# Conditional residual convolutions on one core: the weight products regrouped to eighteen blocks, VectorE's part of S in one form, the residual's identity scaled by ScalarE, and part of G placed ahead of S

## The chip, the cores and the metric

One of the eight cores of one Trainium2 chip runs the kernel. The metric is device time in microseconds (us), the median of several executions; less is better. All numbers are float32.

## What is computed

The reference adds to `x` (128 samples, 64 channels, length 1024) the result of four modulated convolutions of width 3:

```python
s = style @ mw.T + mb                       # per sample, per input channel
weight = SCALE * w * s[:, None, :, None]
demod = rsqrt(sum(weight * weight, axis=(2, 3)) + EPS)
weight = weight * demod[:, :, None, None]
# layers: 'same', 'upsample' (transposed conv, then a 4-tap blur), 'same', 'downsample' (blur, stride 2)
...
return x + chain_of_four_layers(x, cond, weights, biases, mod_w, mod_b)
```

All four layers are linear, so for each sample they amount to one convolution with nine taps of 64 x 64 and a constant; only the first and last three positions differ.

## The kernel before

The 128 samples are taken in 32 units of four samples (`NQ` = 32). A unit's two pairs lie on the two halves of the partitions, and two samples of each half on the two halves of TensorE's columns, so each product is issued as four matmuls of 64 x 64, one for each quarter of the array; "a product" below means these four. Each float32 matmul appears twice in the trace, as two passes.

For each unit the nine taps are built in a chain on TensorE, with a scaled copy after each link:

- `scale3`: ScalarE scales layer 3's weights into `wd` (five blocks of 64 columns: three taps and two sums).
- S (`stage1_a`, `stage1_b`): layer 2's weights times `wd` into the PSUM tile `psS`. ScalarE copies four blocks to `S` after part a; after part b VectorE adds the sums to two blocks (L442) and GpSimd finishes a third (L445). `share_sums` (L462, VectorE) adds blocks of `S` in pairs.
- R (`stage2`, `stage2_rest`): the blurred layer 1 (`E`, nine taps; `Ed`, differences of them) times `S` into `psR`. Some products are common to two blocks of R; they are made apart (`share`, into the free columns behind 340 of a unit's convolution bank `psA`) and copied into `psR` by ScalarE, each to two blocks (`share_copy`, L490), on top of which the rest is accumulated. ScalarE copies `psR` to `R`, GpSimd adds sums of neighbours (`r_sums`, L588).
- W (`stage3_b`, `stage3_a`): layer 0's weights times `R`, part b into a `psA` bank pair that isn't in use yet and part a into `psW`; ScalarE copies to `Wf`, nine blocks, one for each tap.
- H (`combine_a`, `combine_b`): VectorE makes the three combinations of taps that a fast convolution of three outputs with five products (numbered 0 to 4) needs (L662), and `residual` (L659) adds the scaled identity for `x + ...`.

`psS`, `psR` and `psW` are successive uses of one PSUM tile (`ps_w`, one buffer): whoever writes the next waits until the last was read.

The input's side: `G` (`in_g2`, `in_g01`: VectorE, L662) and `T` (`in04`, L740, and `in3`, L711: VectorE; `in1`, L726, and `in2`, L731: GpSimd) are sums of the input's three planes. The convolution itself is five products of three groups each, 340 columns wide (L753): product 3, 1 and 2 into `psA`, 4 into the PSUM tile `Y`, and 0 into the `psA` of the unit. `copy_m3`, `sum1` and `sum2` (VectorE; `sum2` writes `Y` in two steps of 340) form the three output planes, which ScalarE scales (`output`, L830) and SyncE stores.

The order is written out by hand: `turn_of(q)` for q = 4 to 28 works on four units at a time (q's outputs, n = q + 1, c = q + 2, s = q + 4), and each engine executes its instructions in the order of that code. Turns 5 to 27 use `share` (`sharing`). Most turns carry a small side task of VectorE (`SIDE`): one step of 384 to 576 columns in turns 8, 9, 11, 12, 16, 17 and 20 to 27, two or four small ones in turns 5, 6, 7, 10, 13, 15 and 18. Turns 10, 14, 15 and 19 also have products for the edges on TensorE (`SLOTS`), turns 4 to 6 a small constant product (`small`).

Of the kernel before, what the change touches and what calls it, by code (L numbers as in the profile page):

```python
# [63 lines left out]
def kernel(  # L64
# [199 lines left out]
    def var_newton(bs, ls=slice(0, NL)):  # L264
# [5 lines left out]
    tA, tB, tBn, tC, t0, t3, td, tb = (  # L270
        const.tile([P, NQ, 2], F32, name=n) for n in ("tA", "tB", "tBn", "tC", "t0", "t3", "td", "tb")
# [94 lines left out]
    w2n = const.tile([P, 5, C], F32, name="w2n")  # L366

    def split_weights():
        nc_g.tensor_copy(w3x[:, :K], w3)
        nc_g.tensor_scalar_mul(w2n[:, :K], woi[2], -1.0)  # L370
        for t, src in ((w3x, w3), (w2n, woi[2])):
            nc_g.tensor_add(t[:, K:], src[:, : K - 1], src[:, 1:])
# [32 lines left out]
    EVEN = slice(0, K, 2)  # L405

    def stage1(q, pool=None, engs=(nc_a, nc_a), between=None):

        wd = chain[q]
        ps = unit(pool or ps_w, f"psS{q}")  # L410
        for k, (at, at1) in enumerate(((0, 3), (3, 1), (1, 4))):
            tap_matmul(ps, wd, at, 2, woi[2][:, k, :], EVEN, first=k == 0)
            tap_matmul(ps, wd, at1, 1, woi[2][:, k, :], slice(1, 2), last=k == K - 1)
        if between:
            between()
        st, _ = s_tiles(q)
        for r in range(2):
            scaled_copy(engs[r], flat(st[r][:, 1:6]), ps[r][:, : 5 * C], tB[:, q, r : r + 1])
        chain[q] = st
        return ps  # L420

    def stage1_a(q, ps=None):
# [3 lines left out]
        tap_matmul(ps, wd, 2, 2, w2n[:, 0, :], EVEN, first=True)  # L426
        tap_matmul(ps, wd, 3, 2, w2n[:, 2, :], EVEN)
        tap_matmul(ps, wd, 1, 1, w2n[:, 1, :], slice(1, 2))
        st, t = s_tiles(q)
        for r in range(2):  # L430
            scaled_copy(nc_a, flat(st[r][:, :4]), ps[r][:, C : 5 * C], tBn[:, q, r : r + 1])
        chain[q] = wd, ps, st, t

    def stage1_b(q):

        wd, ps, st, t = chain[q]
        tap_matmul(ps, wd, 2, 1, w2n[:, 3, :], slice(3, 4))
        tap_matmul(ps, wd, 4, 1, w2n[:, 4, :], slice(4, 5), last=True)
        for r in range(2):
            p1 = st[r][:, 0:1, :].to_broadcast([P, 2, C])  # L440
            sums = ps[r][:, 2 * C : 6 * C].rearrange("c (a b o) -> c a b o", a=2, b=2)[:, :, 0]
            nc_v.scalar_tensor_tensor(  # L442
                st[r][:, 4:6, :], sums, tB[:, q, r : r + 1], p1, op0=ALU.mult, op1=ALU.subtract
            )
        nc_g.tensor_add(t[:, :, 2], t[:, :, 2], t[:, :, 0])  # L445
        chain[q] = st
        whole[q] = t

    whole, shared_ps = {}, {}
# [3 lines left out]
    def tap_differences():  # L453
# [4 lines left out]
        nc_g.tensor_sub(Ed[:, 4:], E[:, 3:8:4], E[:, 5:6].to_broadcast([P, 2, C]))  # L458

    def share_sums(q):  # L460
        t = whole[q]
        nc_v.tensor_add(t[:, :, 6:8], t[:, :, 1:5:3], t[:, :, 2:6:3])  # L462
# [13 lines left out]
    def share(q, ps):  # L476

        at = [NB + 4 + i * C for i in range(3)]
        p12, p34 = ([b[:, i:j] for b in ps] for i, j in zip(at, at[1:]))
        chain_matmul(p12, E[:, 2], chain[q], slice(6, 7))  # L480
        chain_matmul(p34, E[:, 6], chain[q], slice(6, 7))
        chain_matmul(p34, E[:, 5], chain[q], slice(7, 8), True)
        shared_ps[q] = [b[:, at[0] : at[2]] for b in ps]

    def share_copy(q):

        ps = unit(ps_w, f"psR{q}")
        for r in range(2):
            src = shared_ps[q][r].rearrange("c (a o) -> c a o", a=2)
            nc_a.copy(  # L490
                ps[r][:, C : 5 * C].rearrange("c (a b o) -> c a b o", a=2, b=2),
                src[:, :, None, :].to_broadcast([P, 2, 2, C]),
# [3 lines left out]
    def stage2_rest(q):  # L496

        ps = shared_ps.pop(q)
        block = lambda i, n=1: [b[:, i * C : (i + n) * C] for b in ps]
        apart = [b[:, : 4 * C].rearrange("c (a b o) -> c a b o", a=2, b=2)[:, :, 0] for b in ps]  # L500
        plan = (
            (apart, E[:, 0], slice(1, 4, 2)),
            (block(1), Ed[:, 0], slice(2, 3)),
            (block(2), Ed[:, 1], slice(1, 2)),
            (block(3), E[:, 2], slice(3, 4)),
            (block(3), Ed[:, 2], slice(2, 3)),
            (block(4), Ed[:, 3], slice(1, 2)),
            (block(4), E[:, 4], slice(3, 4)),
            (block(5, 2), E[:, 8], slice(2, 4)),
            (block(5), E[:, 6], slice(3, 4)),  # L510
            (block(1, 2), E[:, 1], slice(4, 6)),
            (block(2), E[:, 3], slice(4, 5)),
            (block(3), Ed[:, 4], slice(5, 6)),
            (block(4), Ed[:, 5], slice(4, 5)),
            (block(5), E[:, 7], slice(5, 6)),
# [5 lines left out]
    def stage2(q, pool=None, engs=(nc_a, nc_a), between=None):  # L521
# [28 lines left out]
    TAPS = slice(3, 9, 2), slice(4, 9, 2), slice(0, 3)  # L550
# [1086 lines left out]
```

## Time and profile before

| | |
|---|---|
| runs | 480.28, 480.38, 481.21 us; median 480.38 |
| profiled execution | span 478.0 us; its own time is not given beside the span |
| granted TensorE clock | 0.997 |
| TensorE matmul busy | 469.6 us (98%) |
| VectorE busy | 417.5 us (87%) |
| ScalarE busy | 310.1 us (65%) |
| GpSimd busy | 163.5 us (34%) |

The span runs from the first to the last instruction. The shares are means over the whole span, and a matmul counts as busy until its modelled end, so 98% does not say that nothing waits. What a turn can be is read from one turn's rows.

### The profile page before, as it was taken

How to read it: one execution, taken by the hardware profiler on the slowest of the kernel's cores; microseconds unless marked ns; L12 is line 12 of the kernel's file. 1: busy time of each engine (PE TensorE's matmuls, PEld its weight loads, DVE VectorE, ACT ScalarE, POOL GpSimd, SP SyncE). 2: the span in 40 equal slices, each digit the busy share in tenths (PEclk: the TensorE clock that was granted, in tenths of full speed). 3: DMA queues.
4: the chain of work that ended last, by engine and by line, in shares of the span. 5: the costliest groups of instructions: out<-in, count | busy, mean ns of one | idle time of the engine just before them, and what ended most of it. 6: DMA issues, size and time to landing. Idle time of an engine off the chain costs nothing.

```text
span 478.0 us, 26721 instructions
## 1 busy us (share of the span) xinstructions
PE 469.6 (98%) x11928; PEld 346.4 (72%) x11928; DVE 417.5 (87%) x690; ACT 310.1 (65%) x708; POOL 163.5 (34%) x197
## 2 busy tenths in 40 slices
PE   8999999999999999999999999999999999999995
PEld 7877788777878876677776677766887777766652
DVE  5889998879889998899979899979989999999895
ACT  5565666667666676666667666667666768766352
POOL 3434032663335342243432233422434432333200
PEclk9999999999999999999999999999999999999998
DMA  5406365544445554345543455533455554445125
GB/s 175 158 28 200 114 195 192 150 139 144 139 150 157 173 173 127 122 151 160 171 149 120 131 170 152 173 127 126 145 169 162 162 154 146 152 146 170 61 91 191
DMA packets 50514, 70.70 MB, mean 148 GB/s; under 512 B 5664, under 2 KB 47328, under 8 KB 50400
## 3 DMA queue, kind: packets, MB, share of 16 engines
q1 hardware_dynamic: 49808, 68.32, 45.8%
q8 instruction: 93, 1.52, 1.5%
q10 hardware_dynamic: 592, 0.69, 0.5%
q14 instruction: 21, 0.17, 0.1%
HBM read 35.36 MB, written 33.62 MB: 144 GB/s over the span
## 4 chain that ended last, share of the span: by engine, by line
PE 95%; DVE 4%; issue 0%; ACT 0%; ACTq 0%; DVEq 0%
PE psA L753 45%; PE Y L753 11%; PE psR L467 9%; PE psA L571 7%; PE psW L571 7%; PE psS L389 6%; PE psR L533 4%; PE psA L467 2%; PE Y L994 2%; DVE H L662 1%; PE Y L180 1%; PE Y L336 1%; DVE G L662 0%; PE psM L204 0%; DVE o L832 0%
## 5 line engine op out<-in xcount | busy, mean ns | idle before, releaser
L753 PE MATMUL psA<-T,H 64*64 64x340 f32 x2304 | 187.3, 447 | 0.8 <-DVE y L662 0.7
L753 PEld LDWEIGHTS psA<-T,H 64*64 64x64 f32 x2304 | 89.9, 133 | 50.0 <-issue 3.1
L662 DVE SCALAR_TENSOR_TENSOR G<-X 128x1376 f32<-128x1376 f32 (+2 forms) x65 | 78.1, 1207 | 1.1 <-DMA X<-in_x 0.9
L726 POOL TENSOR_TENSOR T<-G 128x684 f32<-128x684 f32 x28 | 46.5, 1659 | 73.1 <-DVE G L662 73.1
L445 POOL TENSOR_TENSOR S<-S 128x128 f32<-128x128 f32 x28 | 22.1, 790 | 144.1 <-ACT S L360 136.8
L360 ACT ACTIVATE R<-psR,tC 128x448 f32<-128x448 f32 x63 | 36.5, 630 | 46.3 <-PE psR L467 26.7
L753 PE MATMUL psA<-T,Wf 64*64 64x340 f32 x768 | 63.9, 446 | 0.0
L753 PE MATMUL Y<-T,Wf 64*64 64x340 f32 x768 | 62.8, 451 | 0.1
L662 DVE SCALAR_TENSOR_TENSOR Y<-m,psA 128x340 f32<-128x340 f32 x64 | 33.1, 517 | 28.0 <-PE psA L753 26.6
L360 ACT ACTIVATE psW<-psA 128x128 f32<-128x128 f32 x100 | 19.3, 269 | 50.3 <-PE psA L571 46.2
L740 DVE TENSOR_TENSOR T<-G 128x1368 f32<-128x1368 f32 (+1 forms) x33 | 50.7, 1540 | 0.0
L360 ACT ACTIVATE Wf<-psW,t 128x256 f32<-128x256 f32 (+2 forms) x76 | 32.7, 479 | 26.5 <-PE psW L571 26.2
L711 DVE TENSOR_TENSOR T<-X 128x684 f32<-128x684 f32 x32 | 47.9, 1496 | 0.0
L467 PE MATMUL psR<-S,E 64*64 64x64 f32 (+1 forms) x1472 | 46.5, 238 | 0.0
L731 POOL TENSOR_TENSOR T<-G 128x684 f32<-128x684 f32 x28 | 46.5, 1660 | 0.0
L389 PEld LDWEIGHTS psS<-wd,w2n 64*64 64x64 f32 x1120 | 35.0, 133 | 13.3 <-ACT S L360 0.8
L467 PEld LDWEIGHTS psR<-S,E 64*64 64x64 f32 x1472 | 39.6, 134 | 5.2 <-ACT psR L490 0.2
L753 PEld LDWEIGHTS Y<-T,Wf 64*64 64x64 f32 x768 | 29.6, 132 | 18.0 <-DVE Y L662 0.7
L830 ACT ACTIVATE o<-psA,tb,td 128x340 f32<-128x340 f32 x63 | 37.0, 647 | 6.3 <-PE psA L753 6.3
L753 PEld LDWEIGHTS psA<-T,Wf 64*64 64x64 f32 x768 | 29.1, 133 | 15.1
L830 ACT ACTIVATE o<-Y,tb,td 128x340 f32<-128x340 f32 x63 | 36.6, 637 | 4.5 <-PE Y L753 2.7
L830 ACT ACTIVATE o<-y,tb,td 128x340 f32<-128x340 f32 x62 | 38.5, 679 | 0.6 <-DVE y L812 0.6
(165 smaller groups left out, 832.4 us busy)
## 6 DMA issues: line engine op xcount, KB each, us to landing
out<-o SPq DMA_DIRECT2D x167, 170.0 KB, 2.6
X<-in_x SPq DMA_DIRECT2D x150, 172.0 KB, 3.6
X<-in_x SPq DMA_DIRECT2D x14, 516.0 KB, 5.3
out<-o SPq DMA_DIRECT2D x6, 510.0 KB, 5.4
out<-o SPq DMA_DIRECT2D x2, 340.0 KB, 3.0
Xe<-in_x_ends SPq DMA_DIRECT2D x1, 512.0 KB, 6.7
out<-o ACTq DMA_DIRECT2D x3, 170.0 KB, 2.3
par<-in_params SPq DMA_DIRECT2D x2, 192.0 KB, 3.4
```

The lines of the kernel that those rows point to most:

```text
L360: nc_a.activation(dst, src, AF.Copy, scale=f)
L389: nc.tensor.matmul(ps[r][cols, at * C : (at + n) * C], weight[rows], wd[c if r == 0 else 1 - c][rows, taps], start=first, stop=last, skip_ ...
L445: nc_g.tensor_add(t[:, :, 2], t[:, :, 2], t[:, :, 0])
L467: nc.tensor.matmul(dst[r][cols], weight[rows], st[c if r == 0 else 1 - c][rows, slots, :], start=False, stop=last, skip_group_check=True,)
L571: nc.tensor.matmul(dst[r][cols], weight[rows], t[rows, c, slots, :], start=first, stop=last, skip_group_check=True,)
L662: nc_v.scalar_tensor_tensor(out, x, f, y, op0=ALU.mult, op1=op)
L711: nc_v.tensor_sub(t[:, pairs, 0, :NJ], plane(X, 3, pairs), plane(X, 1, pairs))
L726: eng.tensor_add(t[:, :, 0, :NJ], plane(g, 2), plane(g, 1))
L731: eng.tensor_sub(t[:, :, 1, :NJ], plane(g, 2), plane(g, 1))
L740: nc_v.tensor_sub(t[:, pairs, :, :NJ], both(a, PL), both(b, 1))
L753: nc.tensor.matmul(ps[s][cols, :NB], w, Ts[q, tag][rows, c, i, g : g + NB], start=(g == 0 and m == 3), stop=(g == K - 1), skip_group_check ...
L830: nc_a.activation(dst, src, AF.Identity, bias=add, scale=d3)
```

## The change

The diff, cut to what the prediction speaks of. Blocks of `S` lie in another order (their slots), signs that were in `w2n` and `tBn` go to `En` (negated odd taps of `E`), `Wf` has its taps in natural order, and the PSUM tiles of R start one block further on.

```diff
     def stage1_b(q, eng=nc_v):
...
         for r in range(2):
-            p1 = st[r][:, 0:1, :].to_broadcast([P, 2, C])
-            sums = ps[r][:, 2 * C : 6 * C].rearrange("c (a b o) -> c a b o", a=2, b=2)[:, :, 0]
+            at = slice(3, 6, 1 if eng is nc_v else 2)
+            sums = blocks(ps, at)[r]
+            n = sums.shape[1]
+            p1 = st[r][:, 0:1, :].to_broadcast([P, n, C])
             nc_v.scalar_tensor_tensor(
-                st[r][:, 4:6, :], sums, tB[:, q, r : r + 1], p1, op0=ALU.mult, op1=ALU.subtract
+                st[r][:, at, :], sums, tB[:, q, r : r + 1], p1, op0=ALU.mult, op1=ALU.add
             )
-        nc_g.tensor_add(t[:, :, 2], t[:, :, 2], t[:, :, 0])
+        if eng is not nc_v:
+            eng.tensor_add(t[:, :, 4], t[:, :, 4], t[:, :, 0])
...
     def share(q, ps):
-        at = [NB + 4 + i * C for i in range(3)]
+        p12, p34 = (blocks(ps, slice(i, i + 1)) for i in SHARED)
...
+    SHARED = 5, 6
+    pshare = const.tile([P, 2, 2, C], F32, name="pshare")
...
+    def share_out(q, ps):
+        for r, src in enumerate(blocks(ps, slice(SHARED[0], SHARED[1] + 1))):
+            nc_a.copy(pshare[:, r], src)
     def share_copy(q):
-            src = shared_ps[q][r].rearrange("c (a o) -> c a o", a=2)
+                pshare[:, r, :, None, :].to_broadcast([P, 2, 2, C]),
...
     def r_sums(q, eng):
         t = chain[q]
-        eng.tensor_add(t[:, :, 7:9], t[:, :, 2:6:3], t[:, :, 3:7:3])
+        for r in (slice(0, 2),) if eng is nc_v else PAIR:
+            eng.tensor_add(t[:, r, 7:10], t[:, r, 0:6:2], t[:, r, 1:7:2])
...
-    def stage3_b(q, ps):
+    def stage3_b(q, ps, ahead):
         plan = (
-            (slice(0, 3), w0s[2][:, 2, :], slice(0, 7, 3)),
-            (slice(0, 2), w0s[2][:, 1, :], slice(1, 5, 3)),
-            (slice(0, 2), w0s[2][:, 0, :], slice(2, 6, 3)),
-            (slice(3, 4), w0s[0][:, 0, :], slice(0, 1)),
-            (slice(4, 5), w0s[1][:, 0, :], slice(1, 2)),
-            (slice(4, 5), w0s[1][:, 1, :], slice(0, 1)),
-            (slice(5, 7), w0s[0][:, 1, :], slice(7, 9)),
+            (slice(3, 4), w0s[1][:, 2, :], slice(5, 6)),
+            (slice(3, 4), w0s[1][:, 1, :], slice(6, 7)),
+            (slice(4, 5), w0s[2][:, 2, :], slice(6, 7)),
+            (slice(0, 3), woi[0][:, 1, :], slice(7, 10)),
         )
+            if ahead and i == len(plan) - 1:
+                share(ahead, ps)
...
-        src = blocks(ps, slice(5, 7))
-        for i, f in enumerate((1.0, 1.0 / 3.0)):
-            for dst, v in zip(blocks(pw, slice(i, i + 3, 2)), src):
-                scaled_copy(nc_a, dst, v, f)
-        stage3_out(q, ps, 0, 5)
+        same_row(blocks(pw, slice(0, 1)), woi[0][:, 0, :], t, slice(0, 1))
+        for r in range(2):
+            src = ps[r][:, : K * C].rearrange("c (a o) -> c a o", o=C)
+            dst = pw[r][:, C : 7 * C].rearrange("c (a b o) -> c a b o", b=2, o=C)
+            nc_a.copy(dst, src[:, :, None, :].to_broadcast([P, K, 2, C]))
+        for r, src in enumerate(blocks(ps, slice(3, 5))):
+            scaled_copy(nc_a, Wq[q][0][:, 7:9, r], src, t0[:, q, r : r + 1])
+        if ahead:
+            share_out(ahead, ps)
     def stage3_a(q):
         plan = (
-            (slice(0, 3, 2), Wd[:, 0], slice(3, 7, 3)),
-            (slice(0, 3, 2), w0s[0][:, 2, :], slice(1, 5, 3)),
-            (slice(1, 4, 2), Wd[:, 1], slice(2, 6, 3)),
-            (slice(1, 2), w0s[1][:, 0, :], slice(4, 5)),
+            (slice(1, 6, 2), Wd[:, 0], slice(1, 6, 2)),
+            (slice(2, 7, 2), Wd[:, 1], slice(0, 5, 2)),
+            (slice(2, 7, 2), woi[0][:, 0, :], slice(2, 7, 2)),
+            (slice(3, 6, 2), woi[0][:, 2, :], slice(1, 4, 2)),
         )
-        stage3_out(q, pw, 5, 4)
+        for kind, scale in enumerate((t0, t0b, t0c)):
+            at = slice(kind, 7, K)
+            for r, src in enumerate(blocks(pw, at)):
+                scaled_copy(nc_a, Wq[q][0][:, at, r], src, scale[:, q, r : r + 1])
...
+    def identity(q):
+        for r in range(2):
+            nc_a.activation(x3[:, r], idn3, AF.Copy, scale=t3[:, q, r : r + 1])
-    def residual(q):
+    def residual(q, made):
+        if made:
+            v = W[:, tap(1, 1)]
+            nc_v.tensor_add(v, v, x3)
+            return
...
-    def sum2(q, steps=(0, 1)):
+    def sum2(q, steps=(0, 1), wide=True):
         if 0 in steps:
             m3 = m3c.pop(q)
-            for s, a in enumerate(banks(q)):
-                sum_of(Y[:, s, :NB], m3[:, s], 3.0, a[:, :NB])
+            whole = parts(q) if wide else [(s, a[:, :NB]) for s, a in enumerate(banks(q))]
+            for s, a in whole:
+                sum_of(Y[:, s, :NB], m3[:, s], 3.0, a)
...
     def turn_of(q):
         stage2(c)
+        if not entry:
+            identity(n)
+            if s < NQ:
+                scale3(s)
...
-        stage3_b(c, open_a(n))
+        stage3_b(c, open_a(n), c + 1 if sharing(q) else 0)
...
         conv3(n)
+        copy_m3(n)
         if entry:
-            copy_m3(n)
-        outputs(q, 2)
+            outputs(q, 2)
+        else:
+            conv0(q, 0)
         if s < NQ:
             stage1_a(s)
         if not entry:
-            copy_m3(n)
+            outputs(q, 2)
         in04(n)
-        if sharing(q):
-            share_sums(c + 1)
         in_g2(c)
+        if not entry:
+            in_g01(c)
         side(SIDE, q)
-        conv0(q, *((2,) if entry else range(K)))
+        conv0(q, *((2,) if entry else (1, 2)))
         if entry:
             conv1(n, 0, 1)
-        outputs(q, 1)
+            outputs(q, 1)
         if s < NQ:
             stage1_b(s)
-        in_g01(c)
+        if sharing(q + 1):
+            share_sums(s)
+        if entry:
+            in_g01(c)
         if sharing(q):
-            share(c + 1, banks(q))
             share_copy(c + 1)
+        if not entry:
+            outputs(q, 1)
         outputs(q, 0)
         if q in SLOTS:
+            conv1(n, 0, 1)
             slot(matmuls, width, Y_banks)
...
         in1(c, nc_g)
-        if s + 1 < NQ:
-            scale3(s + 1)
```

VectorE in turn 17, from `in04` to `in3`, before. `G19` is made in two steps (plane 2, then planes 0 and 1), `Ue1` is the turn's side task, `S21` VectorE's part of S.

```order
L740 TENSOR_TENSOR T04_18_5361<-G18_5094 128x4x342
L462 TENSOR_TENSOR S20_5086<-S20_5086 128x2x128
L662 SCALAR_TENSOR_TENSOR G19_5364<-X1_108 128x2x342
L1043 SCALAR_TENSOR_TENSOR Ue1_165<-b1s_145,Ue1_165 128x64x9
L442 SCALAR_TENSOR_TENSOR S21_5356<-psS21_0_5342,tB_134,S21_5356 128x128
L442 SCALAR_TENSOR_TENSOR S21_5356<-psS21_1_5343,tB_134,S21_5356 128x128
L662 SCALAR_TENSOR_TENSOR G19_5364<-X1_108 128x2x688
L662 SCALAR_TENSOR_TENSOR y1_18_5427<-psA18_5249,m3_18_5359 128x680
L711 TENSOR_TENSOR T3_19_5429<-X1_108 128x2x342
```

The same place now:

```order
L773 TENSOR_TENSOR T04_18_5277<-G18_5013 128x4x342
L695 SCALAR_TENSOR_TENSOR G19_5279<-X1_108 128x2x342
L695 SCALAR_TENSOR_TENSOR G19_5279<-X1_108 128x2x688
L1078 SCALAR_TENSOR_TENSOR Ue1_169<-b1s_148,Ue1_169 128x64x9
L451 SCALAR_TENSOR_TENSOR S21_5269<-psS21_0_5255,tB_134,S21_5269 128x192
L451 SCALAR_TENSOR_TENSOR S21_5269<-psS21_1_5256,tB_134,S21_5269 128x192
L474 TENSOR_TENSOR S21_5269<-S21_5269 128x2x2x64
L695 SCALAR_TENSOR_TENSOR y1_18_5326<-psA18_5154,m3_18_5249 128x680
L744 TENSOR_TENSOR T3_19_5328<-X1_108 128x2x342
```

The long step of G (688 columns of each of two pairs) and with it the side task now stand ahead of the two steps of S, which are 192 columns wide instead of 128; the sums of S (L462, now L474) have moved behind them and are those of the same unit.

ScalarE in turn 17, from the copies of S to those of R, before; `psR20` is the copy of the shared products, `o17` the outputs, `wd22` layer 3's scaled weights.

```order
L360 ACTIVATE S21_5356<-psS21_0_5342,tBn_135 128x256
L360 ACTIVATE S21_5356<-psS21_1_5343,tBn_135 128x256
L792 COPY m3_18_5359<-psA18_5249 128x680
L830 ACTIVATE o17_5337<-y1_17_5157,tb_140,td_139 128x340 x2
L490 COPY psR20_0_5407<-psA17_4979 128x256
L490 COPY psR20_1_5408<-psA17_4979 128x256
L830 ACTIVATE o17_5337<-psA17_4979,tb_140,td_139 128x340 x2
L360 ACTIVATE wd22_0_5433<-w3x_141,tA_133 128x320
L360 ACTIVATE wd22_1_5435<-w3x_141,tA_133 128x320
L360 ACTIVATE R20_5493<-psR20_0_5407,tC_136 128x448
```

The same place now; `pshare` is the new SBUF tile of the shared products.

```order
L825 COPY m3_18_5249<-psA18_5154 128x680
L361 ACTIVATE S21_5269<-psS21_0_5255,tB_134 128x4x64
L361 ACTIVATE S21_5269<-psS21_1_5256,tB_134 128x4x64
L864 ACTIVATE o17_5272<-Y_122,tb_141,td_140 128x340 x2
L503 COPY psR20_0_5302<-pshare_145 128x256
L503 COPY psR20_1_5303<-pshare_145 128x256
L864 ACTIVATE o17_5272<-y1_17_5060,tb_141,td_140 128x340 x2
L864 ACTIVATE o17_5272<-psA17_4888,tb_141,td_140 128x340 x2
L361 ACTIVATE R20_5388<-psR20_0_5302,tC_135 128x448
```

The scaled weights are gone from here (they follow R now), and two pairs of outputs, those of `y1` and of `psA`, stand behind the copy of the shared products instead of one.

More of the change, by code (lines that the diff above doesn't have):

```diff
@@ L410, in stage1 @@
         ps = unit(pool or ps_w, f"psS{q}")
-        for k, (at, at1) in enumerate(((0, 3), (3, 1), (1, 4))):
-            tap_matmul(ps, wd, at, 2, woi[2][:, k, :], EVEN, first=k == 0)
-            tap_matmul(ps, wd, at1, 1, woi[2][:, k, :], slice(1, 2), last=k == K - 1)
+        plain.add(q)
+        for k in range(K):
+            tap_matmul(ps, wd, k, K, woi[2][:, k, :], slice(0, K), first=k == 0, last=k == K - 1)
         if between:
@@ L673, in combine_a @@
         sum_of(h1, c, -2.0, a)
-        residual(q)
+        residual(q, made)
         sum_of(h3, h1, 1.0 / 6.0, b)
@@ L1474, in turn_of @@
             small(q)
-        conv1(n, *((2,) if entry else range(K)))
+        conv1(n, *((2,) if entry or q in SLOTS else range(K)))
         sum1(n)
```

141 lines of the change are left out of this document (74 added, 67 removed).

## The prediction

> **What bounds the kernel now.** I read the page's shares and chain first, then one turn's windows, then that turn's rows engine by engine.
>
> ```profile
> span 478.0 us, 26721 instructions
> PE   469.6 (98%) x11928; PEld 346.4 (72%) x11928; DVE 417.5 (87%) x690; ACT 310.1 (65%) x708; POOL 163.5 (34%) x197
> ...
> PE 95%; DVE 4%; issue 0%; ACT 0%; ACTq 0%; DVEq 0%
> ```
>
> TensorE is nearly all of the chain of waits. So products that go away are a gain only while nothing else becomes the pace. The windows show a plain turn (17) and one with edge products (15):
>
> ```profile
> 249.76:265.23 15.47, 15.47 (x412) 10.94 (x408) 12.65 (x24) 9.84 (x23) 4.80 (x5) 1.00 0.46 135
> 279.09:292.93 13.84, 13.84 (x388) 9.80 (x384) 12.94 (x19) 9.85 (x23) 4.83 (x5) 1.00 0.52 157
> ```
>
> In turn 17 TensorE is busy throughout, VectorE for 12.94 of 13.84 us. I count times from the first W product, 279.09. TensorE's rows:
>
> ```profile
> 279.09 0.94 PE L571 MATMUL psA<-R,w0s 64*64 64x192 f32 x24
> 279.85 0.29 PE L571 MATMUL psA<-R,par 64*64 64x64 f32 x8
> ...
> 282.66 0.40 PE L571 MATMUL psW<-R,wsq 64*64 64x128 f32 x8
> 282.88 0.29 PE L571 MATMUL psW<-R,w0s 64*64 64x64 f32 x8
> 283.00 1.90 PE L753 MATMUL psA<-T,H 64*64 64x340 f32 x24
> 284.71 0.73 PE L389 MATMUL psS<-wd,w2n 64*64 64x128 f32 x24
> ...
> 287.56 1.90 PE L753 MATMUL psA<-T,H 64*64 64x340 f32 x24
> 289.28 0.40 PE L467 MATMUL psR<-S,E 64*64 64x128 f32 x8
> ...
> 291.22 1.90 PE L753 MATMUL psA<-T,H 64*64 64x340 f32 x24
> ```
>
> From start to start a product of 64 columns takes 0.12 us (282.88 to 283.00), of 128 0.22, of 192 0.32 (279.09 to 279.85 holds one of 192 and two of 128), three groups of 340 take 1.71, all of R 1.94 (289.28 to 291.22).
>
> VectorE, ScalarE and GpSimd in the same turn:
>
> ```profile
> 279.34 1.07 DVE L662 SCALAR_TENSOR_TENSOR Y<-m,psA 128x340 f32<-128x340 f32 x2 [0.76 <-PE psA L753]
> 280.32 0.85 DVE L812 TENSOR_TENSOR y<-y,psA 128x680 f32<-128x680 f32 x1
> 281.09 0.57 DVE L662 SCALAR_TENSOR_TENSOR H<-Wf 128x384 f32<-128x384 f32 x1
> 281.59 0.47 DVE L659 SCALAR_TENSOR_TENSOR Wf<-idn,t,Wf 128x64 f32<-128x64 f32 x2
> 282.09 0.56 DVE L662 SCALAR_TENSOR_TENSOR H<-H,Wf 128x384 f32<-128x384 f32 x1
> ...
> 284.22 1.58 DVE L740 TENSOR_TENSOR T<-G 128x1368 f32<-128x1368 f32 x1
> 285.71 0.42 DVE L462 TENSOR_TENSOR S<-S 128x256 f32<-128x256 f32 x1
> 286.05 0.87 DVE L662 SCALAR_TENSOR_TENSOR G<-X 128x684 f32<-128x684 f32 x1
> 286.83 1.01 DVE L1043 SCALAR_TENSOR_TENSOR Ue<-b1s,Ue 128x576 f32<-128x576 f32 x1
> 287.76 0.60 DVE L442 SCALAR_TENSOR_TENSOR S<-psS,tB,S 128x128 f32<-128x128 f32 x2
> 288.29 1.58 DVE L662 SCALAR_TENSOR_TENSOR G<-X 128x1376 f32<-128x1376 f32 x1
> 289.78 0.85 DVE L662 SCALAR_TENSOR_TENSOR y<-psA,m 128x680 f32<-128x680 f32 x1
> 290.56 1.85 DVE L711 TENSOR_TENSOR T<-X 128x684 f32<-128x684 f32 x1
> ```
>
> ```profile
> 285.48 0.84 ACT L360 ACTIVATE S<-psS,tBn 128x256 f32<-128x256 f32 x2 [0.32 <-PE psS L389]
> ...
> 288.19 0.63 ACT L490 COPY psR<-psA 128x256 f32<-128x256 f32 x2
> 288.72 1.18 ACT L830 ACTIVATE o<-psA,tb,td 128x340 f32<-128x340 f32 x2
> 289.77 1.02 ACT L360 ACTIVATE wd<-w3x,tA 128x320 f32<-128x320 f32 x2
> 291.51 1.16 ACT L360 ACTIVATE R<-psR,tC 128x448 f32<-128x448 f32 x2 [0.71 <-PE psR L467]
> ```
>
> ```profile
> 279.59 1.66 POOL L731 TENSOR_TENSOR T<-G 128x684 f32<-128x684 f32 x1
> 286.39 0.83 POOL L445 TENSOR_TENSOR S<-S 128x128 f32<-128x128 f32 x1 [5.15 <-ACT S L360]
> 290.03 1.65 POOL L726 TENSOR_TENSOR T<-G 128x684 f32<-128x684 f32 x1 [2.80 <-DVE G L662]
> ```
>
> Here lies a loop that the shares hide. VectorE starts `Y` 0.25 after conv2's end, works without a gap to the S step (8.67), the copy of the shared products into the freed bank ends at 288.82 (9.73), TensorE makes R from 10.19, conv2, and `Y` starts again. Its slack is 10.19 - 9.73 = 0.46 us, with a side task in it.
>
> GpSimd and VectorE hold each other up. `T<-X` takes 1.85 us beside GpSimd's step at 290.03; a VectorE step of that size with GpSimd idle takes 0.87:
>
> ```profile
> L726 DVE TENSOR_TENSOR T<-G 128x684 f32<-128x684 f32 x4 | 3.5, 873 | 0.1
> ```
>
> The side task's 1.01 at 286.83 holds such a wait too: GpSimd's step, issued at 286.39 during G, ran first. By 0.16 us plus 1.04 ns a column (from 684 in 0.87 and 1368 in 1.58) 576 columns need 0.76, of which the next step overlaps 0.09.
>
> **The change, part by part.**
>
> *W's products.* 19 blocks become 18: one of 192, six of 128 and four of 64 become four of 192, one of 128 and four of 64. By the durations that is 2.11 to 1.99: -0.12 us in each of 25 turns, -3.0; three products of 192 for six in each early S (`stage1`) make it -3.1. This is the whole saving on TensorE; S, R and the shared products keep their counts.
>
> *TensorE's times then*, from W's start: three W products, three shared, the sums, one more: 1.14; conv4 to 2.85; W's rest 4.04; conv3 5.75; one group of conv0 6.32; S part a 6.88; two groups 8.02; S part b 8.25; conv1 9.96; R 11.90; conv2 13.61. The same sum for before gives 13.76 where the turn takes 13.84, so a few hundredths are rounding and small waits; I take R as wanted at 9.98.
>
> *The unknown steps.* `Y` in one step of 680: between 0.85 (the step at 289.78, same width) and 1.07 (the two steps it replaces); I take 0.87, giving 0.78 to the next start. Adding `x3` (128 columns): between half of 0.47 and 0.42 (256 columns at 285.71); 0.33 to the next. S in steps of 192: the pair between 0.60 and twice 0.56 (384 columns); +0.13, 0.73. The GpSimd add of S (0.83) is gone. Sums of R on GpSimd, one step of 192 after each half's copy: 0.4 to 0.83 each (S's add, half to all), wanted 0.70 after W's start; R's copies end 0.26 before it (291.51 + 1.16 = 292.67), so hidden at 0.6. ScalarE: four copies of 128, two of 320 and two of 256 become two copies of 384 (0.3 to 0.7 each), two of 128, two to `pshare`, six to `Wf`, two of `x3`: about +1.2 us against 9.85 busy of 13.84; they lie between R and conv3, under conv4 and W's rest (2.9 us). Without that cover each 0.1 would be 0.1 per turn. The shared products, now made in W, need sums of S from the turn before: no wait. Behind the copy of the shared products, which waits for S, now stand four outputs (2.1 us at 0.52, half of 288.72 to 289.77) and R's copies; R's 1.94 and the 0.29 until 291.51 just cover them. SyncE's loads and stores keep their order. No load is wanted before its time: G of planes 0 and 1 moves 2 us forward, on input loaded a turn earlier.
>
> *VectorE's way to S.* The first H stays at 2.00: it waits for GpSimd's step at 279.59 now (its end is 281.25) and would again. Instead of two residual steps (0.50) one (0.33): `T04` starts at 4.96 instead of 5.13. Then 1.49 (284.22 to 285.71), G of plane 2 0.78, and now G of planes 0 and 1, 1.49 (288.29 to 289.78): 8.72. The sums of S (0.34) have left, the side task stays ahead. So S starts at 8.72 in a turn without a side task, 9.39 in turn 17. From S's start to the copy's end is 1.06 now (287.76 to 288.82), 1.19 with wider S. TensorE's first product for the second half of the bank starts 0.11 after R's first, so the copy may end at about 10.04, S start at 8.85. Without a side task this holds by 0.13. With one, TensorE waits for its length minus 0.13.
>
> *Sum of side tasks.* One step of 576 columns (0.67 to the next) in four turns, 0.54 each; of 512 (0.60) in six, 0.47; of 384 (0.47) in two, 0.34; of 448 (0.54) in two, 0.41: 6.5 us. Turn 7's two small steps 0.4. In turns 5 and 6 TensorE wants a constant product right after S part b, at 8.25, and VectorE makes its input and clears its place after G:
>
> ```profile
> 113.75 0.25 DVE L930 TENSOR_TENSOR cc<-Y,a 128x96 f32<-128x96 f32 x1
> ...
> 114.31 0.14 DVE L1454 MEMSET Y<- 128x96 f32 x1
> ```
>
> 0.70 us, so 9.42: 1.2 each, 2.3. Turns 13 and 18 (two steps of 192, four of 64): 0.5 and 0.6. In the slot turns edge products (15.47 - 13.84 = 1.6) cover it. Together 10.3.
>
> *GpSimd behind G.* `in1` starts 0.16 after G of planes 0 and 1 (289.87 to 290.03) and lasts 1.65. That is now in the middle of the side tasks. A single step is already running, and S, which reads PSUM and one tile of SBUF, isn't held up, as `y<-psA,m` isn't (289.78, 0.85 beside GpSimd's step); but a second side step with two SBUF inputs waits some 1.5. Turns 13 and 18: +1.5 each; turns 5 and 6 are a close race, half of 1.5 each; 10 and 15 mostly under their slots, 0.4: 5.0 together.
>
> [...]
>
> *Sum:* 478.0 - 3.1 + 10.3 + 5.0 + 0.4 (turn 28 has no shared products ahead of conv4 and waits for the wide `Y`) = 490.6 us span. The median of the runs is 2.4 above the span: **493**.
>
> **Rivals.**
> 1. *S late, without GpSimd's part* (in1 loses the race to the side steps): 488. For: its start is only 0.16 behind G. Against: the 1.01 at 286.83.
> 2. *A tighter loop*: `Y` at its upper price, or S part b (8.02) waiting for ScalarE's copies of part a, which end 1.06 after part a does (285.26 to 286.32), at 7.94. 0.2 to 0.25 more in some 20 turns: 497 to 498.
> 3. *TensorE keeps the pace, faster.* If S starts at 8.85 or earlier even with side tasks, so 0.5 earlier than summed (the first H not held by GpSimd, 0.2, and shorter overlapped steps), R is never late: -3.1, and up to -0.08 per turn of small waits: 475.5 to 477.3. For: 98% busy now, 0.46 of slack in the loop. Against: 1.49 of G put into a loop from which 0.17 and 0.34 were taken.
> 4. *No change in products' time*: if strided blocks cost more. Against: 64x2x64 products into `psW` (282.66) take the 0.22 of contiguous ones. Below 2%.
>
> **How the numbers follow.** Forecast 0.57, rival 1 0.20, rival 2 0.10, rival 3 0.08, between 3 and no change 0.05. Forecast and rivals 1 and 2 are slower: 0.88, with small delays. Under 0.2% of a change is what a measurement of this kernel can't tell: 0.03; faster 0.09. The range takes the first three and a loop 0.15 slacker in all turns (-3): 484 to 499; outside it 0.16.
>
> **What would show it.** R's first product would start late in turns 8, 9, 16, 17, 20 to 27 by 0.3 to 0.55 us behind conv1's end, released by ScalarE's copy into `psR`, that by S on VectorE; turns of 13 and 18 longer by some 2; turns 12 and 14 to 13.75 at most. Copies into `psR` would show idle time before them ended by VectorE's S (L451). It is wrong if TensorE runs without gaps there, or if ScalarE isn't free in time for R's copies and W starts late, which I count as nothing.

## The result and the profile after

| | before | after |
|---|---|---|
| median of the runs | 480.33 us (480.14 to 481.21) | 497.29 us (496.8 to 497.93) |
| ratio | | 1.0356, 95% interval 1.034 to 1.0373 |
| span of the profiled execution | 478.0 us | 495.5 us |

The change made the kernel slower by 3.6%. The forecast was 493 us, the range 484 to 499. The page of the changed kernel has these lines; the last is the chain of waits.

```profile
span 495.5 us, 25844 instructions
PE 478.0 (96%) x11432; PEld 356.6 (72%) x11432; DVE 412.4 (83%) x642; ACT 349.6 (71%) x852; POOL 159.1 (32%) x198
...
PE 34%; DVE 1%; ACT 0%; DMA 0%; issue 0%; ACTq 0%; DVEq 0%
```

TensorE has 496 fewer matmul records and is busy 8 us longer. The chain, 95% TensorE before, is followed back only into turn 18, and its shares cover a third of the span. The waits say more; these are the ones that concern R and the constant product, in turns 5 to 27 (105 to 450 us; total us, times, longest):

```profile
ACT psR L503 <- DVE S L451: 24.1, 21, 2.7
PEld psR L479 <- ACT psR L503: 12.8, 18, 2.5
PE Y L1274 <- DVE Y L1495: 5.4, 2, 2.9
PE psR L479 <- ACT psR L503: 3.5, 3, 1.9
```

In the same stretch of the kernel before, that view had 0.8 us of issue and no other wait of TensorE's matmuls. Now the copies into `psR` (L503) wait for VectorE's S (L451), and R's weight loads and products (L479) for the copies. Turns 17 and 18 in the windows:

```profile
290.06:304.35 14.29, 14.29 (x374) 10.47 (x371) 12.29 (x17) 11.46 (x31) 4.75 (x5) 1.00 0.47 145
304.35:320.61 16.26, 14.32 (x374) 10.49 (x371) 13.51 (x20) 11.46 (x31) 4.40 (x5) 1.00 0.46 137
```

They took 13.84 and 13.92 before. The rows of turn 17, VectorE, then ScalarE, GpSimd and TensorE, tell how:

```profile
296.66 2.37 DVE L695 SCALAR_TENSOR_TENSOR G<-X 128x684 f32<-128x684 f32 x2
298.95 0.75 DVE L1078 SCALAR_TENSOR_TENSOR Ue<-b1s,Ue 128x576 f32<-128x576 f32 x1
299.62 0.74 DVE L451 SCALAR_TENSOR_TENSOR S<-psS,tB,S 128x192 f32<-128x192 f32 x2
300.39 1.09 DVE L474 TENSOR_TENSOR S<-S 128x256 f32<-128x256 f32 x1
301.41 0.85 DVE L695 SCALAR_TENSOR_TENSOR y<-psA,m 128x680 f32<-128x680 f32 x1
...
300.07 0.70 ACT L503 COPY psR<-pshare 128x256 f32<-128x256 f32 x2 [0.71 <-DVE S L451]
...
299.20 2.00 POOL L759 TENSOR_TENSOR T<-G 128x684 f32<-128x684 f32 x1 [7.02 <-DVE G L695]
...
298.62 1.90 PE L786 MATMUL psA<-T,H 64*64 64x340 f32 x24
300.50 0.76 PE L479 MATMUL psR<-S,E 64*64 64x128 f32 x12
```

Both steps of G and the side task run without a gap into S, which starts at 299.62, 9.56 us after W (8.67 before); the copies end at 300.77. R's first twelve matmuls are spread over 0.76 us, where the first eight took 0.40 before: those of the second half of `psR` start only at 300.82, behind the copy and some 0.5 after the end of conv1's share (298.62 + 1.71).

### The profile page after: what moved, and what is told of

Same layout as the page of the kernel before. It is cut to its first block, busy times and chain, and to the rows that moved or that the text cites. A ratio compares the mean times of both kernels' runs of the same rounds, so it can differ in the third digit from the quotient of the medians.

```text
span 495.5 us, 25844 instructions
## 1 busy us (share of the span) xinstructions
PE 478.0 (96%) x11432; PEld 356.6 (72%) x11432; DVE 412.4 (83%) x642; ACT 349.6 (71%) x852; POOL 159.1 (32%) x198
## 5 line engine op out<-in xcount | busy, mean ns | idle before, releaser
L786 PEld LDWEIGHTS psA<-T,H 64*64 64x64 f32 x2304 | 100.4, 134 | 43.1 <-issue 2.6
L786 PE MATMUL psA<-T,Wf 64*64 64x340 f32 x768 | 68.4, 446 | 0.0
L695 DVE SCALAR_TENSOR_TENSOR Y<-m,psA 128x680 f32<-128x680 f32 (+1 forms) x40 | 29.2, 729 | 46.2 <-PE psA L786 45.9
L361 ACT ACTIVATE Wf<-psW,t 128x192 f32<-128x192 f32 (+1 forms) x76 | 30.0, 445 | 39.4 <-PE psW L585 38.5
L607 POOL TENSOR_TENSOR R<-R 128x192 f32<-128x192 f32 x48 | 28.0, 604 | 76.3 <-ACT R L361 76.3
L479 PEld LDWEIGHTS psR<-S,E 64*64 64x64 f32 x920 | 35.0, 133 | 15.9 <-ACT psR L503 12.8
L479 PE MATMUL psR<-S,E 64*64 64x128 f32 (+1 forms) x920 | 42.3, 246 | 3.5 <-ACT psR L503 3.5
L361 ACT ACTIVATE S<-psS,tB 128x256 f32<-128x256 f32 (+1 forms) x63 | 26.8, 476 | 16.0 <-PE psS L394 16.0
L695 DVE SCALAR_TENSOR_TENSOR H<-H,Wf 128x384 f32<-128x384 f32 x64 | 35.8, 559 | 2.2
L585 PE MATMUL psW<-R,par 64*64 64x128 f32 (+2 forms) x768 | 36.6, 274 | 0.1
```

Source lines behind the costliest of these rows:

```text
L361: nc_a.activation(dst, src, AF.Copy, scale=f)
L479: nc.tensor.matmul(dst[r][cols], weight[rows], st[c if r == 0 else 1 - c][rows, slots, :], start=False, stop=last, skip_group_check=True,)
L585: nc.tensor.matmul(dst[r][cols], weight[rows], t[rows, c, slots, :], start=first, stop=last, skip_group_check=True,)
L607: eng.tensor_add(t[:, r, 7:10], t[:, r, 0:6:2], t[:, r, 1:7:2])
L695: nc_v.scalar_tensor_tensor(out, x, f, y, op0=ALU.mult, op1=op)
L786: nc.tensor.matmul(ps[s][cols, :NB], w, Ts[q, tag][rows, c, i, g : g + NB], start=(g == 0 and m == 3), stop=(g == K - 1), skip_group_check ...
```

## The experiments

In the diffs, `-` is the changed kernel unless another is named. Each is timed against the kernel before on the same chip, whose median lay between 479.8 and 480.2 us.

| | us | ratio to before, 95% | most plain turns |
|---|---|---|---|
| changed kernel | 497.29 | 1.034 to 1.0373 | 14.2 to 14.3 |
| 1: G behind S | 489.58 | 1.0187 to 1.0217 | 14.2 |
| 2: side task behind S | 490.46 | 1.0204 to 1.0233 | 14.2 to 14.3 |
| 3: side task ahead of G | 493.90 | 1.0275 to 1.0303 | 14.2 to 14.3 |
| 4: before, with G ahead of S | 512.01 | 1.0617 to 1.0694 | 14.8 to 14.9 |
| 5: sums and side task behind y<-psA | 482.43 | 1.0032 to 1.0062 | 13.8 to 14.0 |
| 6: turns 5 and 6 alone altered | 490.22 | 1.0171 to 1.0233 | 14.2 to 14.3 |
| 7: 5, with turn 7's side task behind S | 480.38 | 1.0000 to 1.0030 | 13.8 |
| 8: 7, with Y in two steps | 483.48 | 1.0050 to 1.0095 | 14.0 |
| 9: 7, with G behind S | 502.04 | 1.0403 to 1.0492 | 14.3 to 14.7 |

The first four were run with the theory of the prediction, A: G ahead of S is the loss.

**1. G behind S**

```diff
-        if not entry:
-            in_g01(c)
         side(SIDE, q)
...
         if sharing(q + 1):
             share_sums(s)
-        if entry:
-            in_g01(c)
+        in_g01(c)
```

> The changed kernel with one thing put back: G of planes 0 and 1 stands behind the S step and its sums in all turns, as it did before the change. The 18 products, the wide S and Y, the identity by ScalarE and the way of the shared products stay. Theory A (the loss is VectorE's 1.49 us of G placed ahead of the S step, which ScalarE's copy into psR and so R's first product wait for, with what follows from that wait): S starts 1.49 us earlier than now, no product of R waits, GpSimd's in1 no longer meets the side tasks of turns 5, 6, 13 and 18, and what is left is the saving on W, 3.1 us: span 474 to 476, 476 to 478.5 us in the runs, faster than before the change by 2 to 4. Rival B (ScalarE is the pace: 11.46 us busy in turn 17 where it was 9.85, six outputs behind the copy into psR): it does the same work in the same turn, so 488 or more. Rival C (the strided products and copies of W cost more than their columns say): no change against the changed kernel in turns without side tasks, so 490 or more.

489.58 us: theory A fails as the whole story. Rival B's number came, but not by ScalarE, as run 5 shows. R is in time, and still a plain turn takes 14.2. Turn 25's rows of VectorE, GpSimd and TensorE (W starts at 402.04, and the next W at 416.25):

```profile
410.89 0.74 DVE L451 SCALAR_TENSOR_TENSOR S<-psS,tB,S 128x192 f32<-128x192 f32 x2 [0.41 <-PE psS L394]
411.67 0.42 DVE L474 TENSOR_TENSOR S<-S 128x256 f32<-128x256 f32 x1
412.01 1.58 DVE L695 SCALAR_TENSOR_TENSOR G<-X 128x1376 f32<-128x1376 f32 x1
413.51 0.86 DVE L695 SCALAR_TENSOR_TENSOR y<-psA,m 128x680 f32<-128x680 f32 x1
...
413.76 1.64 POOL L759 TENSOR_TENSOR T<-G 128x684 f32<-128x684 f32 x1 [9.21 <-DVE G L695]
415.36 1.78 POOL L607 TENSOR_TENSOR R<-R 128x192 f32<-128x192 f32 x2
...
414.03 0.40 PE L479 MATMUL psR<-S,wsq 64*64 64x64 f32 x14
414.51 1.95 PE L786 MATMUL psA<-T,H 64*64 64x340 f32 x24
```

VectorE now waits 0.41 for TensorE's part b of S. Behind S stand wider S steps, the sums and G, so `y<-psA` ends at 414.37, 12.33 from W's start (11.48 in this turn before), and conv2, which overwrites that `psA`, starts 0.14 after it, some 0.35 late. GpSimd's sums of R end at 417.14, 0.89 after W's start, so W's product of the sums waits too.

**2. The side task behind S**

```diff
-        side(SIDE, q)
+        if entry or q in SMALL:
+            side(SIDE, q)
...
             share_sums(s)
+        if not entry and q not in SMALL:
+            side(SIDE, q)
```

(In turns 5 and 6, `SMALL`, it stands ahead of G of planes 0 and 1.)

> The changed kernel with the side task moved instead of G: G of planes 0 and 1 stays ahead of the S step, and the side task goes behind S and its sums (in turns 5 and 6, where a constant product wants the side task's output, it goes ahead of G of planes 0 and 1, with the clearing of Y). Theory A: S starts at about 8.72 to 8.85 us from W's start, at the edge of what R can take, so R's first product is late by 0 to 0.2 us at most in the turns with a single side step, turns 5 and 6 lose nothing by GpSimd, and the time is 478 to 482: about as before the change, since the loop has no slack left, and so 2 to 4 slower than with G behind S. Rival B (ScalarE): 490 or more. Rival D (any VectorE work between S and y<-psA only moves the delay on, to y<-psA, Y and W): 485 or more, with TensorE waiting for the copy of planes or for W instead of R.

490.46 us: rival D. In most plain turns S starts at 8.77 and R has only the 0.11 to 0.13 between its halves, as expected; the loss moved to conv2. Turn 26 on VectorE and GpSimd:

```profile
425.50 0.74 DVE L451 SCALAR_TENSOR_TENSOR S<-psS,tB,S 128x192 f32<-128x192 f32 x2
426.27 1.42 DVE L474 TENSOR_TENSOR S<-S 128x256 f32<-128x256 f32 x1
...
428.15 0.85 DVE L695 SCALAR_TENSOR_TENSOR y<-psA,m 128x680 f32<-128x680 f32 x1
...
425.75 1.66 POOL L759 TENSOR_TENSOR T<-G 128x684 f32<-128x684 f32 x1 [7.40 <-DVE G L695]
```

The sums of S take 1.42 instead of 0.42: they have two SBUF inputs and end 0.28 after GpSimd's in1 does. The S step beside in1, with one input from PSUM, takes its 0.74.

**3. The side task ahead of G**

```diff
-        if not entry:
-            in_g01(c)
         side(SIDE, q)
         if q in SMALL:
...
+        if not entry:
+            in_g01(c)
```

> The changed kernel with the side task ahead of G of planes 0 and 1 rather than behind it. All the same VectorE work still stands ahead of the S step, so its start is the same in turns with one single side step; what changes is that the side task no longer lies beside GpSimd's in1, and that the constant products of turns 5 and 6 find their input some 1.5 us earlier. Theory A with GpSimd: turns 13 and 18 get shorter by 1.3 to 1.6 us each, turn 5 by some 5 (the 2.89 us wait goes, and with it the stretch in which the granted clock fell to 0.53), turn 6 by 2 to 2.5; the turns with a single side task keep their 0.3 to 0.4: 486 to 488 us. Rival E (GpSimd has nothing to do with it, the side tasks are only late because G stands ahead of S): turns 13 and 18 keep their 15.6 and 16.3 us, and only turns 5 and 6 gain: 490 to 492. Rival B (ScalarE): 495 or more.

493.90 us, a miss, in which the part on GpSimd holds: turn 13 went from 15.64 to 14.27 and turn 18 from 16.26 to 14.80, so -1.4 and -1.5 for the same work in another order. The single side tasks kept theirs. The miss is in turns 5, 6 and 7. In turn 7:

```profile
145.40 0.87 DVE L695 SCALAR_TENSOR_TENSOR G<-X 128x684 f32<-128x684 f32 x1
148.06 0.26 DVE L961 TENSOR_TENSOR oc<-Y,dm 128x96 f32<-128x96 f32 x1 [1.79 <-ACT o L864]
...
150.97 0.76 PE L479 MATMUL psR<-S,E 64*64 64x128 f32 x12 [1.75 <-ACT psR L503]
```

The step that reads the constants waits 1.79 for ScalarE's output of `Y`, which shares the tile, and G and S wait behind it: turn 7 takes 17.62 instead of 14.63. TensorE waits 1.75 for R; the mean granted clock of this execution is 0.995 (0.998 in run 1's). The expectation left out who else reads `Y` at that time.

**4. Before, with G ahead of S** (the kernel before, one thing moved)

```diff
         in_g2(c)
+        if not entry:
+            in_g01(c)
         side(SIDE, q)
...
-        in_g01(c)
+        if entry:
+            in_g01(c)
```

> The kernel from before the change with one thing done: G of planes 0 and 1 stands ahead of the side task and S in all turns but the first, as in the changed kernel. Nothing else of the change is made. Theory A: the sums of S and the second residual step still stand ahead of S there, so its start is later than in the changed kernel by 0.4 to 0.5 us, against narrower S steps (0.13): R's first product is late by 0.5 to 0.9 us in some 18 turns, turns 13 and 18 lose 2 to 3, turns 5 and 6 together 5 to 8, so 496 to 508 us. Rival B or C (ScalarE's work, or W's products, cause the loss): 479 to 483, since neither is in this kernel.

512.01 us. Without any other part of the change, G's place costs 32 us; S starts at 10.1 to 10.3 and R is 0.9 to 1.1 late in the plain turns. Some 5 of the 32 (an estimate from the run's windows: three stretches of 3.4 us at half the clock, in turns 5, 6 and 13) are the clock's. Together with run 1: the old order can't bear G ahead of S, and the new one can't bear it behind.

From here on theory A2: VectorE's chain has two ends for which TensorE waits, S (R's first product) and `y<-psA` (conv2), and in1 holds the steps with two SBUF inputs that stand behind G (1.42 instead of 0.42 in run 2).

**5. The sums of S and the side task behind y<-psA** (`aside` is the side task with the clearing of `Y`)

```diff
         stage2(c)
+        if q - 1 in SMALL and not entry and q - 1 != FIRST:
+            small(q - 1)
...
+        if entry:
+            aside()
...
-        if sharing(q + 1):
-            share_sums(s)
...
+        elif q in SLOTS:
+            aside()
...
-        if q in SMALL:
+        if entry:
             small(q)
...
         sum1(n)
+        if not entry:
+            if sharing(q + 1):
+                share_sums(s)
+            if q not in SLOTS:
+                aside()
         in3(c)
```

> The changed kernel, G still ahead of S, with VectorE's other work put behind sum1: the sums of S and the side task (with the clearing of Y in turns 5 and 6) stand behind the step y<-psA, ahead of in3; in the turns with edge products the side task stands behind S. The constant product of turns 5 and 6 goes behind R of the next turn. Theory A2, formed from the four runs before this one: VectorE's chain has two ends that TensorE waits for, the S step (R's first product) and y<-psA (conv2), and a VectorE step with two SBUF inputs behind G of planes 0 and 1 is held by GpSimd's in1 (the sums of S took 1.42 us there instead of 0.42 when the side task was moved behind them). Here S starts at 8.8 us from W's start, nothing with two SBUF inputs stands between it and y<-psA, so R starts at 10.15, conv2 at about 12.1, and a plain turn takes 13.8 us (before 13.84, the changed kernel 14.2 to 14.3); what W's products save is taken back by conv4, which starts at 1.27 because the wide Y ends at 1.21. Turns 5 and 6 take about 14.2. 478 to 482 us. Rival B (ScalarE's 11.46 us a turn set the pace): 14.2 a turn, 488 or more. Rival F (GpSimd's sums of R are now held by VectorE's side task and in3 and W waits for them): 14.0 to 14.2 a turn, 484 to 488.

482.43 us, 0.4 above the expectation's upper end. Plain turns take 13.79 at best, with ScalarE busy for 11.39 of it in turn 23, so rival B is out. What is too much lies mostly in one place: turn 8 takes 15.73. GpSimd's steps at the end of turn 7 show why:

```profile
147.16 1.29 POOL L284 TENSOR_SCALAR tb<-oc 64x48 f32<-64x48 f32 x2 [10.48 <-DVE oc L962]
148.54 1.65 POOL L759 TENSOR_TENSOR T<-G 128x684 f32<-128x684 f32 x1
150.14 1.46 POOL L607 TENSOR_TENSOR R<-R 128x192 f32<-128x192 f32 x2
```

Turn 7's side task feeds two steps on GpSimd, and in1 and the sums of R stand behind them in its queue.

**6. Turns 5 and 6 alone**

```diff
         stage2(c)
+        if q - 1 in SMALL and not entry and q - 1 != FIRST:
+            small(q - 1)
...
+        if entry or q not in SMALL:
+            aside()
...
             share_sums(s)
+        if not entry and q in SMALL:
+            aside()
...
-        if q in SMALL:
+        if entry:
             small(q)
```

> The changed kernel with turns 5 and 6 alone altered: there the side task and the clearing of Y stand behind the S step and its sums, and the constant product stands behind R of the next turn. All other turns as in the changed kernel. Theory A2: the 2.89 us that TensorE waited in turn 5 for the constant product's cleared place go, and with them the stretch after it in which the granted clock was 0.53; both turns then take about 14.3 us instead of 19.34 and 16.61, and the other turns stay: 489.5 to 491 us. If the low clock had a cause of its own (the time since the start, say, and not the wait), turn 5 would keep some 1.6 us of it: 491.5 to 493. Rival H (the constant product's wait only moves on to R or conv2): turns of 15.5 or more, 493 or more.

490.22 us, as A2 expected, 7.1 less than the changed kernel: the two turns now take 14.92 and 14.12 at a granted clock of 1.00. These are the rows of turn 5 in the changed kernel (VectorE, GpSimd, TensorE), and one of its windows:

```profile
115.42 0.25 DVE L965 TENSOR_TENSOR cc<-Y,a 128x96 f32<-128x96 f32 x1
115.71 1.72 DVE L966 SCALAR_TENSOR_TENSOR cc<-b1s,cc 128x96 f32<-128x96 f32 x1
117.44 0.14 DVE L1495 MEMSET Y<- 128x96 f32 x1
...
115.68 1.63 POOL L759 TENSOR_TENSOR T<-G 128x684 f32<-128x684 f32 x1 [5.13 <-DVE cc L965]
...
117.72 0.42 PE L1274 MATMUL Y<-cc,wsum 64*64 64x96 f32 x2 [2.89 <-DVE Y L1495]
...
118.07 3.29 PE L786 MATMUL psA<-T,H 64*64 64x340 f32 x22
...
117.70:121.10 3.40, 3.38 (x30) 3.09 (x34) 0.87 (x3) 2.91 (x6) 0.00 (x0) 0.53 0.28 93
```

A step of 96 columns takes 1.72 us (0.26 before the change) and ends 0.12 after in1 does; TensorE idles 2.89 us, and then conv1 takes 3.29 (1.90 in turn 17) at about half the clock, 0.53.

**7. Turn 7's side task right behind S** (against run 5)

```diff
-        elif q in SLOTS:
+        elif q in SLOTS or q == 7:
             aside()
...
-            if q not in SLOTS:
+            if q not in SLOTS and q != 7:
                 aside()
```

> The kernel with VectorE's side work behind y<-psA (G still ahead of S, the sums of S behind y<-psA, the constant product behind R), with one more step put back: turn 7's side task stands right behind the S step, ahead of y<-psA, since GpSimd's table steps (L284) wait for it and in1 and the sums of R are queued behind them. Theory A2: turn 8 takes 13.9 us instead of 15.73, nothing else moves: 480 to 481 us, which no measurement here tells from the kernel before the change. If the 15.73 had another cause (the side task of turn 8), it stays: 482 to 483.

480.38 us, as expected. Turn 8 takes 13.88, and a plain turn (25) reads:

```profile
392.96:406.75 13.79, 13.79 (x372) 9.92 (x368) 11.57 (x17) 11.46 (x30) 4.38 (x5) 1.00 0.54 164
...
401.73 0.74 DVE L451 SCALAR_TENSOR_TENSOR S<-psS,tB,S 128x192 f32<-128x192 f32 x2
403.35 0.87 DVE L695 SCALAR_TENSOR_TENSOR y<-psA,m 128x680 f32<-128x680 f32 x1 [0.88 <-PE psA L786]
...
407.08 0.87 DVE L695 SCALAR_TENSOR_TENSOR Y<-m,psA 128x680 f32<-128x680 f32 x1 [1.15 <-PE psA L786]
...
407.78 0.29 PE L585 MATMUL psW<-R,par 64*64 64x64 f32 x8
408.00 1.37 PE L786 MATMUL Y<-T,Wf 64*64 64x340 f32 x16
```

VectorE now waits for TensorE at both of its ends, 0.88 and 1.15 us. The waits that the change brought are gone from most plain turns, and yet the kernel is not faster than before. The last two rows say where much of W's saving went: the product ahead of conv4 needs 0.12 by its columns, and conv4 starts 0.22 after it, 0.05 after `Y` ends (407.95).

**8. Y in two steps** (against run 7)

```diff
-            sum2(q)
+            sum2(q, wide=False)
```

> The same kernel (turn 7's side task right behind S, other side work behind y<-psA) with one part of the change undone: Y is written in two steps of 340 columns instead of one of 680. Theory A2: conv4 waits for the end of that work in every turn, also with the wide step (1.25 us from W's start, where TensorE has 1.14 us of other products ahead of it). Two steps end about 0.2 us later, so conv4 starts at 1.4 to 1.5 and each of some 23 turns takes 0.15 to 0.2 us longer: 484 to 485.5 us. Rival I (conv4 at 1.25 is TensorE's own time, and the products ahead of it take longer than their columns say): no change, 480 to 481.

483.48 us; a plain turn takes 13.99, 0.20 more, as A2 expected (the total is lower than expected by 0.5). TensorE's products up to conv4 are the same, and conv4 follows the end of `Y`, 411.25, by 0.06:

```profile
410.18 1.07 DVE L695 SCALAR_TENSOR_TENSOR Y<-m,psA 128x340 f32<-128x340 f32 x2 [1.15 <-PE psA L786]
...
410.88 0.29 PE L585 MATMUL psW<-R,par 64*64 64x64 f32 x8
411.31 0.80 PE L786 MATMUL Y<-T,Wf 64*64 64x340 f32 x8
```

**9. G behind S** (against run 7)

```diff
-        if not entry:
-            in_g01(c)
...
         elif q in SLOTS or q == 7:
             aside()
+        in_g01(c)
```

> The kernel whose sums of S and side tasks stand behind y<-psA (turn 7's right behind S), with G of planes 0 and 1 put back behind the S step, as before the change. So no step but G stands between S and y<-psA, and S waits for nothing but TensorE. Theory A2: neither R nor conv2 is late (S at 8.3, y<-psA at 10.6 to 11.5, conv2 wanted at 12.1), but GpSimd's in1 starts 1.5 us later, at 10.8, so the sums of S, the side task and in3, with two SBUF inputs each, are held until 12.4 and end at 14 or later; GpSimd's sums of R come after them and W's product of these sums waits: 14.1 to 14.8 us a turn, 487 to 500 us. Rival J (G ahead of S only costs, so that its place behind S is the better one once nothing else stands there): 13.7 to 13.8 a turn, 478 to 480.5 us.

502.04 us, slower than the upper end of A2's range by 2 and far from rival J. Turn 23:

```profile
394.20 1.41 DVE L474 TENSOR_TENSOR S<-S 128x256 f32<-128x256 f32 x1
395.53 0.74 DVE L1115 TENSOR_TENSOR Ue<-Ve 128x576 f32<-128x576 f32 x1
396.19 1.26 DVE L744 TENSOR_TENSOR T<-X 128x684 f32<-128x684 f32 x1
...
395.63 2.27 POOL L607 TENSOR_TENSOR R<-R 128x192 f32<-128x192 f32 x2 [0.31 <-ACT R L361]
...
397.95 0.39 PE L585 MATMUL psA<-R,par 64*64 64x192 f32 x3 [0.52 <-POOL R L607]
```

in1 ends at 395.32, and the sums of S take 1.41 instead of 0.42; then VectorE's `T<-X` takes 1.26 (0.85 in turn 17 of the changed kernel), and beside these steps the sums of R (1.14 there) take 2.27, for which W's product waits. (Turns 14 and 19 take 18.7 and 21.0: there the longer side tasks of the turn ahead end so late that conv4 waits 2.94 and 2.00 us for `Y`; the mean granted clock of this execution is 0.993, in run 7's 0.997.) So G ahead of S is what keeps GpSimd's sums of R free; it paid for its place only when the sums and the side task left VectorE's way.

## Why the prediction was right, and where not

The differences, group by group, of the starts of W's first product in the two traces, beside what the prediction's terms add up to with the 0.12 of W taken off:

| turns | predicted | measured |
|---|---|---|
| 8, 9, 11, 12, 16, 17, 20 to 27 (one side step) | 4.8 | 3.9 |
| 13, 18 | 3.9 | 4.1 |
| 5, 6 | 3.6 | 6.9 |
| 7 | 0.3 | 0.7 |
| 10, 14, 15, 19 (edge products) | -0.1 | 0.6 |
| 28 and all behind it | 0.3 | 1.0 |
| all ahead of turn 5 | -0.2 | 0.3 |
| sum | 12.6 | 17.5 |

- **The loop** (S late, the copy, R): right. R's second half was late by 0.30 to 0.56 in the turns with one side step, against 0.34 to 0.54, released as forecast; run 5 took the side task out of the way and the wait went. That the sizes agree is in part luck, since both ends came later than summed: in turn 17 S at 9.56 instead of 9.39 (`T04` to G takes 1.67, not 1.49), and conv1 at 8.56 instead of 8.25, as conv4 started at 1.39 instead of 1.14 behind the late `Y`. The 3.9 in the table also understates these turns: some of them (11 and 21 above all) took longer than 13.84 before, and against 13.84 a turn the changed kernel's come to 5.0 more.
- **The unknown prices**: the wide `Y` 0.87 (0.87 taken), the S pair 0.74 (0.73), the sums of R 0.57 each, 1.14 for two (0.6). ScalarE's added work, counted as hidden, was, though it came to 1.6 us a turn instead of 1.2: 11.46 us busy in turns of 13.79.
- **GpSimd behind G**: right in turns 13 and 18: the 1.5 taken for each was an estimate from `in1`'s 1.65, and run 3 showed 1.4 and 1.5. That `in1` would also hold the sums of S, which have two SBUF inputs and now stand right behind G, I did not see; it made them 1.09 in turn 17 (0.42 before), and it decides runs 2 and 9.
- **The mis-sized term: turns 5 and 6.** I took GpSimd's hold there as a close race at half its price. In turn 5 it was lost in full (1.72 for 0.26) and the low clock that followed TensorE's wait cost a further 1.4 in conv1 alone, of which the prediction had nothing: +5.0 where half the sum, 1.8, was expected. Turn 6 came out at +1.9.
- **W's saving**: its 3.1 was counted as gained in full, and conv4's wait for `Y` for turn 28 alone. In run 7, with no other wait left, a turn is 0.05 shorter than before instead of 0.12 (conv4 at 1.25 from W's start, summed 1.14). So rival 3's price of 475.5 to 477.3 was wrong too: with S early enough the kernel stands at 480.4, no change that this measurement can tell. Over turns 5 to 27 run 7 is 0.5 us shorter than the kernel before, while its start is 0.3 and turn 28 with all behind it 1.0 longer; no run separates what makes these two longer.
- **Rival 2** has the nearest total (497 to 498), by a mechanism that was not there: `Y` took its lower price, and no copy of part a held part b.
- **Turns 12 and 14** were said to take 13.75 at most: 14.09 and 15.65. That line contradicted the prediction's own sum, in which turn 12 has a side task and turn 14 edge products.
- **Left open**: a few plain turns in runs 5 and 7 (17 and 20) take 0.3 to 0.8 longer than their neighbours by a wait that the profile calls issue.

## What to carry to other kernels

A step that is moved ahead of a deadline moves the whole queue in front of it: list every step that now stands between the engine's last wait and each of its deadlines, and also what the moved step releases on another engine and whom that holds. Put first what another engine waits for, then what only the next turn needs; the same work in that order (run 7) took 480 us, in others 482 to 502. A saving on the engine that sets the pace counts only where it isn't itself waiting; look at each of its starts for the step that it follows by a few hundredths.

## What the runs showed of the hardware

- **The granted clock was about one half after some waits of TensorE and 1.00 after others, and the wait's length alone does not tell which.** In windows behind the waits it was 0.53 after 2.89 us (changed kernel, turn 5, 117.70 to 121.10), 0.55 after 3.18 (run 4, turn 5, 118 to 121), 0.50 after 3.02 (run 4, turn 6, 138 to 140) and 0.50 after 1.96 (run 4, turn 13, 247 to 250), but 1.00 after 2.50 (changed kernel, turn 6, 136 to 141) and 1.00 after 2.56 (run 4, turn 18, 326.2 to 331). The windows of run 4 around the 1.96 us, which ended at 246.04:

```profile
246.00:247.00 1.00, 0.96 (x44) 0.88 (x47) 1.00 (x2) 1.00 (x3) 0.00 (x0) 1.00 0.00 0
247.00:248.00 1.00, 1.00 (x42) 1.00 (x38) 0.97 (x3) 1.00 (x3) 0.00 (x0) 0.50 0.38 124
248.00:249.00 1.00, 1.00 (x38) 1.00 (x34) 0.01 (x1) 0.24 (x1) 0.00 (x0) 0.50 0.19 60
249.00:250.00 1.00, 1.00 (x27) 0.91 (x24) 0.00 (x0) 0.41 (x1) 0.00 (x0) 0.50 0.50 178
250.00:251.00 1.00, 1.00 (x16) 0.95 (x12) 0.00 (x0) 0.75 (x2) 0.17 (x1) 0.79 0.74 121
```

Here the drop comes 1 us after TensorE is busy again and lasts 3.4 us (0.50 in three windows, 0.79 in the fourth). No run shows what decides.

- **Beside GpSimd's in1, VectorE steps with two SBUF inputs took longer, and steps with one input from PSUM did not.** The sums of S took 1.42 us instead of 0.42 (run 2), a step of 96 columns 1.72 instead of 0.26 (changed kernel, turn 5). The S steps took 0.74 beside in1 in run 2 and 0.74 ahead of it in run 1; `y<-psA` took 0.85 beside in1 before the change and 0.85 behind it in the changed kernel (turn 17). There in1 itself, started at 299.20 during the side task (298.95 to 299.70), took 2.00 instead of 1.65.
- **A wait on one half stayed in the turn.** After R's halves started apart, `Y` began 0.46 after W's first product (304.81 in the changed kernel, W at 304.35), where it was 0.25 before.
